# Who asks for a weight, and when: `wo` issued by ScalarE in quarters at the start of a two-layer graph kernel

## The chip, the cores and the metric

The kernel runs on one core of one Trainium2 chip. Its metric is the device time of one execution in microseconds (us), the median of several executions.

## What is computed

The input `x` has 64 batches of 256 rows with 512 features, all float32. `adj` is a 256 x 256 matrix of zeros and ones. Two layers follow each other:

```python
# layer 0: masked attention, 8 heads of 64, then residual and layer norm
q, k, v = (x @ Wq + bq), (x @ Wk + bk), (x @ Wv + bv)        # each (b, 256, 8, 64)
scores  = einsum('bqhd,bkhd->bhqk', q, k) / sqrt(64) + (1 - adj) * -1e9
out     = einsum('bhqk,bkhd->bqhd', softmax(scores), v) @ Wo + bo
x       = layernorm(x + out)
# layer 1: neighbours' sum, one weight, then residual and layer norm
y       = einsum('nm,bmd->bnd', adj, x)
x       = layernorm(x + y @ weight + bias)
```

## The kernel before, in words

**Pairs of batches.** The 64 batches are worked through as 32 pairs. A tile of a pair holds 128 partitions by 512 float32 values. All names below carry the pair, so `x(1, 2)` is the third feature block of pair 1.

**Products in three digits.** A float32 product is made out of three passes over cut numbers in the `fp32r` form. Each operand is split into `high` (a ScalarE copy with a scale), `low` and `diff` (two VectorE operations, L123 and L124 for weights, L288 and L289 for x), and for weights and keys one more ScalarE scaling of `low` (L127, L393). A block of a product is then 4 x 3 = 12 matmuls at L338. `ring_high`, `ring_rest` and `ring_scale` do this for the k-th quarter of a weight; the results go into the pool `wr`, which has six buffers, three for each stage.

**Stages of weights.** `STAGES` lists which digits are in the ring and in what order: the second half of the heads of `wq` and `wk` for pair 0 (`qk1`), then `wv` (`v`, the third weight), then the first half of `wq` and `wk` for pair 1 (`qk0`), and from there on the stages of each pair. The digits of a weight are made once, written to DRAM by GpSimd (`keep`, L132), and read back by GpSimd for each later pair (`load_w`, L110).

**Order of work.** PE, DVE, ACT and POOL run in the order that the program writes out by hand. `start()` is the part that the change touches. It turns pair 0's x on TensorE, makes the products of queries and keys, then `scores(0, 0)` (matmuls L454, exps L469), the products of `v`, `values(0, 0)`, `scores(0, 1)`, and `bv_wo`. A step such as `(ring_rest, "v", 0, 0)` in a list puts its instructions on its engines at that place.

**bv_wo** (L240) multiplies the bias `bv` with `wo` once, so that it can be added to `bo`: four matmuls of 32 columns, one for each quarter of `wo`, each written as two instructions. ScalarE copies the result (L242). `with_bv` (matmul L247, addition L248) adds it to the `bo` tile. After `bv_wo` come two `begun` products, which need only `high` digits, and the products of queries and keys of pair 1 out of the `qk0` digits. `values(0, 1)` (L410, L420) and `scores(1, 0)` follow.

**Loads at the start.** SP issues nearly all of them, in this order: x of pair 0 (L176), columns of `wk` and `wq` (L169), `adj` (L193), `wv` in four parts (L196), x of pair 1 in sixteen parts of 64 KB (L81), `wo` in four quarters of 256 KB (L203, tile `hl`), the biases `bo` and `b1` spread over all partitions (L91), then x of pair 2 and the residual rows (`load_r`, L86). ScalarE issues the first columns of `wq` and the small biases.

**Semaphores of transfers.** In the built program the transfers of SP and ScalarE share eight semaphores, dealt in rotation. A transfer is issued once the previous one with its semaphore has landed.

**adj** is turned by TensorE (`adj_t`, L227), copied into `adjT` by VectorE (L228), and tested once for values other than zero and one (`test_adj`, L232 to L234). **The next rows** are x of pair 1, turned by VectorE (`x_t`, L276).

Of the kernel before, what the change touches and what calls it, by code (L numbers as in the profile page):

```python
# [8 lines left out]
F32 = mybir.dt.float32  # L9
# [6 lines left out]
P = 128  # L16
# [13 lines left out]
def tile_adj_resnorm(tc, x, adj, wq, bq, wk, bk, wv, bv, wo, bo, w1, b1, out):  # L30
    good = fast(tc, x, adj, wq, bq, wk, bk, wv, bv, wo, bo, w1, b1, out)
    with tc.If(good < P):
        general(tc, x, adj, wq, bq, wk, bk, wv, bv, wo, bo, w1, b1, out)


def fast(tc, x, adj, wq, bq, wk, bk, wv, bv, wo, bo, w1, b1, out):
# [6 lines left out]
    nc = tc.nc  # L43
    B, N, D = x.shape
    HD = D // H
    DC = D // P
    NC = N // P
    NP = B // 2
    HF = D // 2
# [12 lines left out]
    two = pool("two", 2)  # L62
# [8 lines left out]
    RAW, SCRATCH, W, UNCUT, BEGUN = {}, {}, {}, {}, {}  # L71
# [3 lines left out]
    def load_x(p, i):  # L75

        if p < NP:

            t = XC[p, i] = two.tile([P, D], F32, name="o" if p == 1 and i > 1 else "x")
            for q in range(4):  # L80
                nc.sync.dma_start(t[q * 32:(q + 1) * 32].rearrange("i (m j) -> i m j", j=32), xb[p, i, q])  # L81
# [7 lines left out]
    def on_all(b, name):  # L89
        t = cpool.tile([P, D], F32, name=name)  # L90
        nc.sync.dma_start(t, b.partition_broadcast(P))  # L91
        return t
# [103 lines left out]
        nc.sync.dma_start(RAW["v", k], wv[k * P:(k + 1) * P])  # L196
    for i in range(4):
        load_x(1, i)
    for k in range(DC):
        if k % 2 == 0:  # L200
            raw_o = two.tile([P, 2, D], F32, name="hl")
        RAW["o", k] = raw_o[:, k % 2]
        nc.sync.dma_start(RAW["o", k], wo[k // 2 * HF:(k // 2 + 1) * HF].rearrange("(h a i) e -> a h i e", h=4, a=2)[k % 2])  # L203
    bo_s, b1_s = on_all(bo, "bo"), on_all(b1, "b1")

    def small_ones():

        nc.gpsimd.memset(power, -0.5)
        nc.gpsimd.memset(first_of_32, 0.0)
        for d in range(DC):  # L210
            nc.gpsimd.memset(first_of_32[d * 32:d * 32 + 1], 1.0)

    def load_l():
        t = two.tile([P, DC, D], F32, name="r")
        nc.sync.dma_start(t, w1.rearrange("(c p) e -> p c e", p=P))
        for k in range(DC):
            RAW["l", k] = t[:, k]
# [223 lines left out]
    def scores(p, g, between=[]):  # L441
        if not 0 <= p < NP:
            return
        for b in range(2):
            for kc in range(NC):

                sc = [banks.tile([P, 2, N], F32, name="ps") for s in range(2)]
                keys = slice(b * N + kc * P, b * N + (kc + 1) * P)
                for a in range(2):
                    digits = (1, 0, 2) if (p, g) != (0, 0) else (0,)  # L450
                    for i in digits:
                        for s in range(2):
                            r = slice(s * HD, (s + 1) * HD)
                            nc.tensor.matmul(sc[s][:, a, :], K[p, g][r, a, i, keys], Q[p, g][r, a, i, b * N:(b + 1) * N],  # L454
                                             start=i == digits[0], stop=i == digits[-1])
                if (p, g) == (NP - 1, 1):

                    names = (("x", two), ("high", four), ("low", four), ("diff", four))
                    name, pool_of = names[2 * b + kc]
                    e = [pool_of.tile([P, 2, N], F32, name=name) for _ in range(2)]  # L460
                    whole = []
                else:
                    e = one.tile([P, 2, 2, N], F32, name=f"e{2 * b + kc}")
                    whole, e = [e.rearrange("p s a n -> p (s a) n")], [e[:, s] for s in range(2)]
                E[p, g, b, kc] = e, whole
                if (b, kc) == (1, 1):
                    do(*between)
                for s in range(2):
                    nc.scalar.activation(e[s], sc[s], AF.Exp, scale=(RHO if (p, g) != (0, 0) else 1.0) * qscale)  # L469
# [15 lines left out]
    def masks(p, g, b):  # L485
        return [(masked, p, g, b, 0), (masked, p, g, b, 1), *([(summed, p, g, b)] if (p, g) != (NP - 1, 1) else [])]
# [145 lines left out]
    def do(*tasks):  # L632
        for t in tasks:
            for f, *args in (t if isinstance(t, list) else [t]):
                f(*args)
# [54 lines left out]
    def steps_of(*args):  # L690

        h, r, s = ([(f, *args, k) for k in range(4)] for f in (ring_high, ring_rest, ring_scale))
        return h[:2], r[:1] + h[2:3] + r[1:2] + h[3:], r[2:3] + s[:1] + r[3:] + s[1:2], s[2:]

    def start():
        make_identity(nc, ident)
        do(*((x_first, i) for i in range(4)), (biases,), *((x_high, 0, i) for i in range(4)), (small_ones,))
        qk1, v = (steps_of(*stage) for stage in STAGES[:2])
        high, rest, scale = ([(f, "qk0", 1, k) for k in range(DC)] for f in (ring_high, ring_rest, ring_scale))
        do((block, "q", 0, 0), (x_rest, 0, 0), (x_rest, 0, 1), qk1[0], (block, "k", 0, 0), (x_rest, 0, 2), (x_rest, 0, 3), qk1[1],  # L700
           (block, "q", 0, 1), qk1[2], v[0], (block, "k", 0, 1), (x_t, 1, 0), (x_t, 1, 1), (adj_t,), qk1[3])
        scores(0, 0)
        do(v[1], masks(0, 0, 0), (block, "q", 0, 2), v[2], (qk_high, "q", 0, 2), (qk_rest, "q", 0, 2), v[3],
           (block, "k", 0, 2), (x_high, 1, 0), (x_high, 1, 1), (qk_high, "k", 0, 2), (qk_rest, "k", 0, 2), masks(0, 0, 1),
           (block, "q", 0, 3), (k_low, 0, 2), (qk_high, "q", 0, 3), (qk_rest, "q", 0, 3), (x_rest, 1, 0), (x_t, 1, 2),
           (block, "k", 0, 3), (stage_end, 0), (qk_high, "k", 0, 3), (qk_rest, "k", 0, 3), (x_rest, 1, 1), (x_t, 1, 3), high[:2],
           (block, "v", 0, 0), (x_high, 1, 2), high[2:], (k_low, 0, 3), (block, "v", 0, 1), (x_rest, 1, 2), (test_adj,),
           (block, "v", 0, 2), (x_high, 1, 3), (x_rest, 1, 3), (block, "v", 0, 3), (stage_end, 0), (load_r, 0), (load_l,))
        values(0, 0)
        scores(0, 1)  # L710
        do((bv_wo,), rest[:2], scale[:1], rest[2:3], scale[1:2], rest[3:], scale[2:])
        qk0 = [(f, name, 1, j) for j in range(2) for name in "qk" for f in (qk_high, qk_rest)]
        m = masks(0, 1, 0) + masks(0, 1, 1)
        do((begun, "q", 1, 0), (begun, "k", 1, 0), (block, "q", 1, 0), m[:4], qk0[:2], (block, "k", 1, 0), m[4:5], qk0[2:4], m[5:],
           (block, "q", 1, 1), (k_low, 1, 0), qk0[4:6], (o_high, 0, 0, 0), (o_high, 0, 1, 0), (o_rest, 0, 0, 0),
           (with_bv,), (block, "k", 1, 1), qk0[6:], (stage_end, 0), (k_low, 1, 1), (o_rest, 0, 1, 0))
# [45 lines left out]
    with tc.manual_schedule(engines={PE, DVE, ACT, POOL}):  # L762
        start()
        first(1, steps_of("o", 0))
        second(1)
        load_r(1)
        for w in range(2, NP - 1):
            first(w)
            second(w)
        ending()  # L770
# [188 lines left out]
```

## Time and profile before

| What | Value |
|---|---|
| median of 3 runs | 2397.47 us (2393.38 to 2397.6) |
| profiled execution | 2397.81 us |
| its span in the profile | 2395.8 us |
| mean granted TensorE clock | 0.998 |
| TensorE (PE) busy | 2376.4 us, 99% |
| weight loads (PEld) busy | 1908.5 us, 80% |
| VectorE (DVE) busy | 1990.7 us, 83% |
| ScalarE (ACT) busy | 1503.4 us, 63% |
| GpSimd (POOL) busy | 440.8 us, 18% |

The span runs from the first to the last instruction; the profiled execution's own time has some 2 us more around it. Busy shares are means over the whole span. A wait shows as idle time ahead of an instruction, and the trace names what ended it.

### The profile page before, as it was taken

Reading aid. Unit: us, or ns where it says so; the run is one execution under the profiler, and the core shown is the slowest. Engines: PE = TensorE matmul, PEld = TensorE weight load, DVE = VectorE, ACT = ScalarE, POOL = GpSimd, SP = SyncE. Lnnn points to the kernel's source line nnn. Section 1 sums busy time; section 2 is a strip of 40 time slices with the busy share of each in tenths; the row PEclk is TensorE's granted clock in tenths of the full one; section 3 lists DMA queues with packets and bytes.
Section 4 is the critical chain, followed back from the end, with each engine's and each line's share of the span. In section 5 each row is a group of like instructions: output and inputs, shape, how many; then the busy total and the mean of one; then the engine's idle time right before and its main releaser. Section 6 shows DMA issues by size and latency. Waiting matters only on the chain.

```text
span 2395.8 us, 42996 instructions
## 1 busy us (share of the span) xinstructions
PE 2376.4 (99%) x16925; PEld 1908.5 (80%) x16925; DVE 1990.7 (83%) x3311; ACT 1503.4 (63%) x2793; POOL 440.8 (18%) x751
## 2 busy tenths in 40 slices
PE   8999999999999999999999999999999999999998
PEld 6788887887878888788887788887888878888777
DVE  7888888898888888888888889888888888888867
ACT  6566566665665666656666566566566665665656
POOL 1121112111111211111111111111121111111121
PEclk9999999999999999999999999999999999999999
DMA  9888788777897777877778877789777887787782
GB/s 290 272 275 251 253 264 295 239 231 259 255 303 247 224 267 255 274 261 239 245 257 264 285 241 235 255 254 310 240 226 265 255 283 259 229 256 258 255 268 68
DMA packets 373091, 608.69 MB, mean 254 GB/s; under 512 B 271500, under 2 KB 275092, under 8 KB 312596
## 3 DMA queue, kind: packets, MB, share of 16 engines
q0 software_dynamic: 70544, 499.15, 56.9%
q1 hardware_dynamic: 301632, 106.34, 20.5%
q8 instruction: 135, 2.21, 0.4%
q14 instruction: 72, 0.59, 0.1%
q10 hardware_dynamic: 708, 0.40, 0.1%
HBM read 551.29 MB, written 49.28 MB: 251 GB/s over the span
## 4 chain that ended last, share of the span: by engine, by line
PE 97%; DMA 2%; SPq 1%; DVE 0%; ACT 0%; issue 0%; POOLq 0%; ACTq 0%
PE ps L338 72%; PE ps L420 9%; PE ps L454 8%; PE ps L614 5%; PE ps L410 3%; DMA hl<-in_L_gnn_Wo_dram 1%; SPq L81 1%; DMA vc<-in_adj_dram 0%; DMA low<-in_x_dram 0%; SPq L203 0%; PE ps L240 0%; PE ps L564 0%; SPq L169 0%; ACT waste L516 0%; PE ps L247 0%
## 5 line engine op out<-in xcount | busy, mean ns | idle before, releaser
L372 ACT ACTIVATE uncut<-ps,numbers 128x512 f32<-128x512 f32 x252 | 173.8, 690 | 275.9 <-PE ps L338 220.1
L475 DVE TENSOR_TENSOR e<-e,adjT 128x1024 f32<-128x1024 f32 x252 | 299.3, 1219 | 0.2 <-ACT e L469 0.2
L338 PE MATMUL ps<-low,wr 128*128 128x512 f32 x992 | 271.4, 395 | 0.0
L338 PE MATMUL ps<-wr,sl 128*128 128x512 f32 x1008 | 270.6, 390 | 0.1
L338 PE MATMUL ps<-wr,sh 128*128 128x512 f32 x1008 | 269.8, 389 | 0.0
L338 PE MATMUL ps<-wr,sd 128*128 128x512 f32 x1008 | 269.4, 389 | 0.0
L338 PE MATMUL ps<-high,wr 128*128 128x512 f32 x992 | 267.0, 391 | 0.0
L338 PE MATMUL ps<-diff,wr 128*128 128x512 f32 x992 | 265.0, 389 | 0.0
L522 POOL TENSOR_TENSOR ln<-ln,numbers 128x2 f32<-128x2 f32 x127 | 140.4, 1105 | 666.7 <-DVE ln L521 615.3
L469 ACT ACTIVATE e<-ps 128x512 f32<-128x512 f32 x504 | 253.0, 626 | 8.9 <-PE ps L454 8.9
L516 ACT ACTIVATE waste<-r,ln 128x512 bf16<-128x512 f32 x255 | 183.4, 719 | 104.7 <-DVE ln L509 98.5
L420 PE MATMUL ps<-e,v 128*32 128x256 f32 x4032 | 229.1, 379 | 0.0
L537 ACT ACTIVATE r<-r,ln 128x512 f32<-128x512 f32 x254 | 193.2, 809 | 55.2 <-DMA x<-in_x_dram 31.4
L338 PEld LDWEIGHTS ps<-wr,sh 128*128 128x128 f32 x1008 | 189.3, 188 | 39.9
L338 PEld LDWEIGHTS ps<-high,wr 128*128 128x128 f32 x992 | 186.6, 188 | 42.7 <-issue 1.7
L338 PEld LDWEIGHTS ps<-wr,sd 128*128 128x128 f32 x1008 | 189.2, 188 | 39.5 <-DMA wr<-o 0.2
L338 PEld LDWEIGHTS ps<-diff,wr 128*128 128x128 f32 x992 | 186.2, 188 | 39.1
L338 PEld LDWEIGHTS ps<-wr,sl 128*128 128x128 f32 x1008 | 186.9, 188 | 38.2 <-issue 0.4
L384 DVE SCALAR_TENSOR_TENSOR qT<-qT,uncut 128x512 fp32r<-128x512 f32 x126 | 86.7, 688 | 154.3 <-ACT qT L377 154.2
L454 PEld LDWEIGHTS ps<-qT,kT 64*128 64x128 f32 x3056 | 187.8, 187 | 26.4 <-PE ps L420 12.3
L338 PEld LDWEIGHTS ps<-low,wr 128*128 128x128 f32 x992 | 177.8, 188 | 35.1 <-PE ps L338 0.2
L454 PE MATMUL ps<-qT,kT 64*128 64x256 f32 x3056 | 201.4, 285 | 0.0
(165 smaller groups left out, 4152.9 us busy)
## 6 DMA issues: line engine op xcount, KB each, us to landing
wr<-qk POOLq DMA_DIRECT2D x183, 1024.0 KB, 7.8
wr<-v POOLq DMA_DIRECT2D x93, 1024.0 KB, 6.7
wr<-o POOLq DMA_DIRECT2D x90, 1024.0 KB, 8.1
wr<-l POOLq DMA_DIRECT2D x90, 1024.0 KB, 8.5
r<-in_x_dram SPq DMA_DIRECT2D x32, 1024.0 KB, 12.3
out_dram<-r SPq DMA_DIRECT2D x62, 512.0 KB, 2.9
x<-in_x_dram SPq DMA_DIRECT2D x488, 64.0 KB, 5.7
qk<-wr POOLq DMA_DIRECT2D x6, 1024.0 KB, 7.1
```

The source lines that it names most:

```text
L338: nc.tensor.matmul(pm, *pairs[k][i], start=i == 0 and k == 0, stop=i == n - 1 and k == DC - 1)
L372: nc.scalar.activation(to, pm, AF.Identity, bias=bias[:, j:j + 1], scale=scale)
L384: nc.vector.scalar_tensor_tensor(low, high.bitcast(F32), -RHO, UNCUT.pop((name, p, j)), op0=OP.mult, op1=OP.add)
L410: nc.tensor.matmul(at[h * 32:(h + 1) * 32, b, :], ones, chunk[h], start=i == 0, stop=i == len(sm) - 1)
L420: nc.tensor.matmul(at[h * 32:(h + 1) * 32, a, :], V[p, b][:, kc, col:col + 32], E[p, g, b, kc][0][h % 2][:, h // 2, :], start=kc == 0, sto ...
L454: nc.tensor.matmul(sc[s][:, a, :], K[p, g][r, a, i, keys], Q[p, g][r, a, i, b * N:(b + 1) * N], start=i == digits[0], stop=i == digits[-1])
L469: nc.scalar.activation(e[s], sc[s], AF.Exp, scale=(RHO if (p, g) != (0, 0) else 1.0) * qscale)
L475: nc.vector.tensor_tensor(e, e, mask[:, kc:kc + 1, :].to_broadcast([P, e.shape[1], N]), op=OP.mult)
L516: nc.scalar.activation(waste, R[p][b][:, c], AF.Square, bias=t[0][:, c:c + 1], accum_out=t[1][:, c:c + 1])
L522: nc.gpsimd.tensor_tensor(t[2], t[1], power[:, cs], op=OP.pow)
L537: nc.scalar.activation(r[:, :cut], r[:, :cut], AF.Identity, scale=scale, bias=bias)
L614: nc.tensor.matmul(pm[:, j, :], t[:, i, mc, j * P:(j + 1) * P], adjT[:, mc, :], start=mc == 0 and i == 0, stop=mc == NC - 1 and i == 1)
```

## The change

The quarters of `wo` are no longer issued by SP between x of pair 1 and the biases. A new step `load_o` issues one quarter from ScalarE's queue; four such steps stand in `start()`. In VectorE's order, the digits of the first quarter of `wv` go ahead of the copy of `adj`, the transpose of x(1, 1) goes behind the digits of the second quarter, and `test_adj` moves from behind x(1, 2)'s digits to ahead of the keys' third block, `(block, "k", 0, 2)`. In the new kernel `load_o` stands at L208 to L212, and the lines behind it are one higher than before (L338 becomes L339).

```diff
-    for k in range(DC):
-        if k % 2 == 0:
-            raw_o = two.tile([P, 2, D], F32, name="hl")
-        RAW["o", k] = raw_o[:, k % 2]
-        nc.sync.dma_start(RAW["o", k], wo[k // 2 * HF:(k // 2 + 1) * HF].rearrange("(h a i) e -> a h i e", h=4, a=2)[k % 2])
     bo_s, b1_s = on_all(bo, "bo"), on_all(b1, "b1")
...
+    def load_o(k):
+        if k % 2 == 0:
+            RAW["o"] = two.tile([P, 2, D], F32, name="hl")
+        RAW["o", k] = RAW["o"][:, k % 2]
+        nc.scalar.dma_start(RAW["o", k], wo[k // 2 * HF:(k // 2 + 1) * HF].rearrange("(h a i) e -> a h i e", h=4, a=2)[k % 2])
...
-        do((block, "q", 0, 0), (x_rest, 0, 0), (x_rest, 0, 1), qk1[0], (block, "k", 0, 0), (x_rest, 0, 2), (x_rest, 0, 3), qk1[1],
-           (block, "q", 0, 1), qk1[2], v[0], (block, "k", 0, 1), (x_t, 1, 0), (x_t, 1, 1), (adj_t,), qk1[3])
+        do((load_o, 0), (block, "q", 0, 0), (x_rest, 0, 0), (x_rest, 0, 1), qk1[0], (load_o, 1), (block, "k", 0, 0), (x_rest, 0, 2), (x_rest, 0, 3),
+           qk1[1], (load_o, 2), (block, "q", 0, 1), qk1[2], v[0], (block, "k", 0, 1), (x_t, 1, 0), v[1][:1], (load_o, 3),
+           (adj_t,), qk1[3])
         scores(0, 0)
-        do(v[1], masks(0, 0, 0), (block, "q", 0, 2), v[2], (qk_high, "q", 0, 2), (qk_rest, "q", 0, 2), v[3],
+        do(v[1][1:], (x_t, 1, 1), masks(0, 0, 0), (block, "q", 0, 2), v[2], (qk_high, "q", 0, 2), (qk_rest, "q", 0, 2), v[3], (test_adj,),
            (block, "k", 0, 2), (x_high, 1, 0), (x_high, 1, 1), (qk_high, "k", 0, 2), (qk_rest, "k", 0, 2), masks(0, 0, 1),
...
-           (block, "v", 0, 0), (x_high, 1, 2), high[2:], (k_low, 0, 3), (block, "v", 0, 1), (x_rest, 1, 2), (test_adj,),
+           (block, "v", 0, 0), (x_high, 1, 2), high[2:], (k_low, 0, 3), (block, "v", 0, 1), (x_rest, 1, 2),
```

## The prediction, made before the changed kernel ran

> **What bounds it now.** First the page: TensorE is busy 99% of the span, and the chain that ended last is TensorE for 97%. Two per cent of that chain is DMA, and its largest piece is `wo` (tile `hl`).
>
> ```profile
> PE 2376.4 (99%) x16925; PEld 1908.5 (80%) x16925; DVE 1990.7 (83%) x3311; ACT 1503.4 (63%) x2793; POOL 440.8 (18%) x751
> ...
> PE 97%; DMA 2%; SPq 1%; DVE 0%; ACT 0%; issue 0%; POOLq 0%; ACTq 0%
> ```
>
> So look where TensorE waits: the waits of TensorE in 0 to 90 us name one large one, and the chain in order of time (start, length) shows its place.
>
> ```profile
> PE ps L240 <- DMA hl<-in_L_gnn_Wo_dram: 6.5, 1, 6.5
> PE ps L260 <- DMA low<-in_x_dram: 4.1, 2, 3.8
> ...
> 30.48 32.98 DMA hl<-in_L_gnn_Wo_dram
> 63.45 0.04 issue
> 63.50 1.91 PE ps L240 x2
> 65.41 8.90 PE ps L338 x36
> 74.31 0.86 PE ps L247 x2
> 75.17 2.76 PE ps L338 x12
> ```
>
> The fourth quarter of `wo` is issued at 30.48 us and lands 33 us later; `bv_wo` (L240) has done three quarters and waits for it. The timeline of TensorE (start, length, names, idle time before), then the windows of 3 us (TensorE busy first, its clock in the third column from the end), give the price.
>
> ```profile
> 55.98 1.06 PE L240 MATMUL ps<-hl,numbers 128*32 128x512 f32 x6
> 63.50 1.91 PE L240 MATMUL ps<-hl,numbers 128*32 128x512 f32 x2 [6.46 <-DMA hl<-in_L_gnn_Wo_dram]
> ...
> 77.86 1.07 PE L410 MATMUL ps<-sm,ones 128*32 128x256 f32 x16
> ```
>
> ```profile
> 57.00:60.00 3.00, 0.04 (x3) 0.00 (x0) 2.93 (x6) 0.96 (x2) 0.00 (x0) 0.95 0.41 132
> 60.00:63.00 3.00, 0.00 (x0) 0.00 (x0) 2.97 (x3) 0.00 (x0) 0.54 (x1) 0.50 0.72 282
> 63.00:66.00 3.00, 2.50 (x4) 0.75 (x5) 1.54 (x2) 0.50 (x2) 0.00 (x0) 0.50 0.70 216
> 66.00:69.00 3.00, 3.00 (x14) 2.46 (x13) 0.00 (x0) 2.17 (x5) 0.53 (x1) 0.92 0.45 78
> ```
>
> The stall also halves TensorE's clock until about 66 us. After 90 us the waits view names none of TensorE at all, so time saved here reaches the end.
>
> **The Trainium skill.** "TensorE: Matmul & The Clock Gate", Part 1 (the HAM clock gate): an idle window of about 3.4 us gates the array to half clock, and as long a busy one frees it. The trace agrees: 0.50 in 60 to 66 us, 1.00 after 69. "DMA: Bandwidth & Descriptors", section on queues, rings and completion order: SP and ACT own one queue row each, and every DMA engine goes round the rows packet by packet. From 30 to 57 us the trace gives GpSimd's q0 72.6% and SP's q1 19.6%, which fits `wo` crawling behind 3 MB of weight copies. Same page, "Issuing engines are not separate DMA queues": another issuer brings no bandwidth. No run yet shows the effect of that. Same page, on the anatomy of one DMA: semaphore waits happen on the issuing sequencer; here SP's issues stand so.
>
> **The change, part by part.**
>
> *Gain.* From `bv_wo` at 55.98 to `values(0,1)` at 77.86 TensorE takes 21.88 us. Its work there: eight `bv_wo` matmuls, 1.06 for six plus 0.35 for two, 1.4; 48 matmuls L338 at 0.227 (a block of 12 is 2.72, from the starts of its groups), 10.9; L247 0.86. Sum 13.2, so 8.7 us are lost: 6.46 idle, 1.91 - 0.35 = 1.56 and 12.52 - 11.76 = 0.76 at half clock.
>
> *When `wo` lands now.* ScalarE issues the quarters at about 12, 15, 18 to 19 and 23 us, against 28.4 to 30.5. Even with the old 33 us the last lands at 57, where it is needed; 25 to 45 us is likelier, as far less stands ahead of it in its row.
>
> *What is late next.* ScalarE's four scalings of the qk0 digits (L127) follow its eight exps and the `bv_wo` copy. Exps end at 57.96, the copy at 58.55, then 0.55 each: 59.1, 59.65, 60.2, 60.7. TensorE, after eight `begun` matmuls, wants the first at 59.2 and the fourth at 59.9: 0.8 lost. VectorE's share of the digits is done at 59.7. From 59.2, with 0.8 of stall, the 40 matmuls left (9.1) and L247 (0.86) bring `values(0,1)` to 70.0 instead of 77.86: 7.86 gained.
>
> *VectorE behind it.* It loses its 6.67 us idle time before L384 (64.54 to 71.21). Contiguous work of 9.77 us from there to 80.98 now ends at 74.2; ScalarE's `k_low` adds 0.63, so 74.8. `scores(1,0)` starts 4.46 after `values(0,1)`, at 74.5, and wants the second half of the keys 0.4 later. A tie: 0 to 0.3, I take 0. Further on VectorE had 1.47 idle at 96.3, enough.
>
> *ScalarE's four issues.* Each is a queue instruction of 0.3 to 0.7 us (ACTq's old ones 0.26 to 0.58, SP's of 256 KB 0.43 to 1.05), plus a wait. Hardware-queue transfers share eight semaphores in rotation, and an issue waits for its semaphore's previous transfer. The built program shows these waits: quarter 0 for the second half of `wq` (landed 11.86), quarter 1 for `wv` 0 (14.7), quarter 2 for `wv` 3 (17.5), quarter 3 for quarter 1. Queued behind each is the copy out of a TensorE product, and TensorE waits for that copy. ScalarE's room:
>
> ```profile
> 12.19 0.69 ACT L372 ACTIVATE qT<-ps,numbers 128x512 f32<-128x512 f32 x1 [1.44 <-PE ps L338]
> ...
> 15.62 0.69 ACT L372 ACTIVATE kT<-ps,numbers 128x512 f32<-128x512 f32 x1 [1.71 <-PE ps L338]
> ...
> 19.06 0.69 ACT L372 ACTIVATE qT<-ps,numbers 128x512 f32<-128x512 f32 x1 [1.71 <-PE ps L338]
> ...
> 22.49 0.69 ACT L372 ACTIVATE kT<-ps,numbers 128x512 f32<-128x512 f32 x1 [0.67 <-PE ps L338]
> ...
> 24.11 4.00 ACT L469 ACTIVATE e<-ps 128x512 f32<-128x512 f32 x8
> ```
>
> The first two fit to 0.2 us (11.86 and 14.7, plus 0.5). For the third, 512 KB of new traffic at the windows' 370 GB/s push `wv` 3 by 1.4 to 18.9; issued by 19.4 it makes the copy at 19.06 late by 0.35, less than the 0.67 idle before 22.49. The score matmuls feel it only if `wv` 3 lands after 19.3. The fourth delays the exps by 0.5; TensorE needs the first bank back at 26.47, so 1.6 may go. I book 0.2 for all four; bounds 0 and 2. Below nothing is excluded here: nothing on this path becomes earlier.
>
> *SP's queue.* It loses four issues (28.41 to 31.52), so `bo`, `b1`, x(2,..) and R follow sooner. But semaphores are dealt anew: x(1,0)'s last part waits for `wv` 1, x(1,1)'s third part for quarter 0, x(1,2)'s last for quarter 2, `bo` for quarter 3. `bo` is wanted by `with_bv` at 72.2 (it landed at 64.1 before), x(1,2) at 43.9: nothing booked. GpSimd's copies keep their order and meet 1 MB more traffic earlier; their landings have over 5 us of room before TensorE's use.
>
> *VectorE's order.* The transpose of x(1,1), which stood 2.86 idle until 23.42, goes behind the digits of `wv` 1 and `adj`'s copy. With x landing some 2 later, x(1,0)'s transpose comes at 21.5, one digit pair (1.33) to 23.5, `adj` to 24.2; the last scores need its bank at 25.4: covered, 1.2 to spare. The `adj` test (three operations, 1.0) moves from 49.1 into the 1.51 idle at 34.87, and frees 1.0 at 50 that ends at `vc` (53.65) anyway: at most 0.15 of it counts. All else moved costs nothing, because TensorE runs without a gap from 26.5 to 57.
>
> *Sum.* 7.86 - 0.2 = 7.7. Against the profiled execution (2397.81; span 2395.8, 2.0 around it) that is 2390.1; the median, 2397.47, is 0.34 lower, so 2389.8.
>
> **Rivals.** (A) *Less is gained:* the waits on `wv` 3 or quarter 1 hold ScalarE 1 to 3 us past its room, or VectorE decides at the keys. For it: the room is 0.7 and 1.6. Gain 3 to 6, time 2391.5 to 2394.5. (B) *Slower:* quarter 3's wait for quarter 1 stands ahead of the exps. If quarter 1 needs the 33 us that a quarter took in SP's queue, it lands at 49; the exps start there and not at 25.7 at latest, 23 us of stall against 7.9 saved: about 2413. It decides from a landing after 33 us. Against it: quarter 1 is issued before GpSimd's copies (17.66), in a row of its own. (C) *No change:* quarter 3 lands as late as before, starved by q0, or `bo` behind it holds `with_bv` until the old time: about 2396 to 2398. Against it: it starts 7 us earlier.
>
> **Numbers.** Forecast 0.62, A 0.21, C 0.10, B 0.07. A measurement of this kernel tells some 0.2% (4.8 us) from no change, and one of the three times shown is 2393.38. The forecast's own range is 2387 to 2391.5; with most of A it is 2387 to 2394. Faster by over 0.2% is below 2392.7: the forecast and most of A, 0.78. Same: the rest of A and C, 0.15. Slower: B, 0.07.
>
> **What would show it.** Right: no wait of L241 for `hl`, clock 1.00 throughout 57 to 69, `values(0,1)` near 70.2 (77.86), four DMA issues on ACTq with the copy L373 late by under 0.7, VectorE unbroken from 64 to 74. A gap before the score matmuls (L455) at 23 to 26 us would show A or B; a wait at L241 or before L249 shows C. The prediction is wrong if TensorE gets a new idle stretch over 3 us before 90 us, or the gain is outside 3.5 to 10.5.

## The result: slower, 1.0027 times the time before

The changed kernel takes 2402.87 us (median; 2399.82 to 2407.7) against 2397.47 us in the same set of runs. The ratio is 1.0027, with a 95% interval of 1.0017 to 1.0036: slower by about 4 to 9 us, where 2389.8 was predicted. Its profiled execution, at 2400.37 us (span 2398.4), is among its faster ones, and so shows only 2.6 of these microseconds.

The page first. TensorE's busy time and share have hardly moved, and DMA has gone from the chain that ended last; VectorE has come in.

```profile
PE 2377.4 (99%) x16925; PEld 1909.5 (80%) x16925; DVE 1990.3 (83%) x3311; ACT 1502.3 (63%) x2793; POOL 439.4 (18%) x751
...
PE 96%; DVE 1%; ACT 0%; issue 0%; POOLq 0%; ACTq 0%
```

The waits of TensorE in 0 to 100 us (total, times, longest) name what took the place of `wo`. There is no wait for `hl` any more, and a new one of 7.4 us for `adjT`.

```profile
PE ps L455 <- DVE adjT L229: 7.4, 1, 7.4
...
PE ps L455 <- ACT kT L394: 0.5, 1, 0.5
```

TensorE's timeline gives the places. The last six matmuls of `scores(0,0)` stand still from 25.9 to 33.35; `bv_wo` then runs as one piece of 1.06 us.

```profile
22.65 3.29 PE L455 MATMUL ps<-qT,kT 64*128 64x256 f32 x26
33.35 2.07 PE L455 MATMUL ps<-qT,kT 64*128 64x256 f32 x6 [7.42 <-DVE adjT L229]
...
66.16 1.06 PE L241 MATMUL ps<-hl,numbers 128*32 128x512 f32 x8
...
79.45 1.07 PE L411 MATMUL ps<-sm,ones 128*32 128x256 f32 x16
...
84.99 2.78 PE L455 MATMUL ps<-qT,kT 64*128 64x256 f32 x42 [0.46 <-ACT kT L394]
```

The windows (TensorE busy first, its clock third from the end) show that the half clock moved along with the stall: from 60 to 66 us in the kernel before to 27 to 38 us here.

```profile
27.00:30.00 3.00, 0.00 (x0) 0.00 (x0) 0.00 (x0) 2.44 (x5) 0.53 (x1) 0.65 0.47 132
30.00:33.00 3.00, 0.00 (x0) 0.00 (x0) 2.28 (x4) 1.62 (x4) 0.00 (x0) 0.50 0.91 354
33.00:36.00 3.00, 2.65 (x8) 1.72 (x9) 1.59 (x3) 1.14 (x3) 0.00 (x0) 0.50 0.50 145
...
63.00:66.00 3.00, 3.00 (x52) 2.91 (x48) 2.81 (x6) 2.50 (x5) 0.65 (x2) 1.00 0.62 262
```

`adjT` is late because VectorE, ahead of it, waits 10.86 us for the first rows of pair 1. Its timeline:

```profile
30.69 0.71 DVE L277 STREAM_TRANSPOSE xT<-x 128x512 f32<-128x512 f32 x1 [10.86 <-DMA x<-in_x_dram]
31.32 0.65 DVE L123 SCALAR_TENSOR_TENSOR wr<-wr,high 128x512 fp32r<-128x512 f32 x1
32.01 0.69 DVE L124 SCALAR_TENSOR_TENSOR wr<-wr 128x512 fp32r<-128x512 f32 x1
32.62 0.68 DVE L229 CAST adjT<-ps 128x512 fp32r<-128x512 f32 x1
```

In the kernel before, x(1,0) was turned at 19.86 without a wait and `adj` copied at 24.06:

```profile
19.86 0.71 DVE L276 STREAM_TRANSPOSE xT<-x 128x512 f32<-128x512 f32 x1
...
24.06 0.65 DVE L228 CAST adjT<-ps 128x512 fp32r<-128x512 f32 x1
```

SP's timeline shows the same x in its queue: the eight issues of x(1,0) and x(1,1), before and then after.

```profile
10.49 8.12 SPq L81 DMA_DIRECT2D x<-in_x_dram  x8
```

```profile
11.18 17.00 SPq L81 DMA_DIRECT2D x<-in_x_dram  x8
```

It is not the issues that make x(1,0) late. Its four parts were issued by 16.2 us, against 15.0 before; the last of them landed at 30.66, against 18.85 (a landing is the last update of the transfer's semaphore in the trace).

**The balance**, read from the start of the first sums matmul (L410, after L411) in each `values` block. The table holds the changed kernel and all experiments; x(1,0)'s column shows lateness only where VectorE reaches its transpose early, so not in 8 and 9, where it stands further back. Differences are to the profile of the kernel before, ratios to its runs in the same set (medians 2396.9 to 2397.5).

| Kernel | Time, us | Ratio (95%) | x(1,0) turned at | values(0,0) | values(0,1) | values(1,0) |
|---|---|---|---|---|---|---|
| before | 2397.47 | 1 | 19.9 | 48.46 | 77.86 | 118.25 |
| changed | 2402.87 | 1.0027 (1.0017-1.0036) | 30.7 | +10.17 | +1.58 | +2.31 |
| 1 order alone | 2398.13 | 1.0005 (0.9996-1.0014) | 19.9 | +0.01 | +1.32 | +1.33 |
| 2 issue alone | 2406.69 | 1.0041 (1.0027-1.0055) | 26.4 | +16.25 | +7.66 | +8.86 |
| 3 quarter 3 later | 2403.54 | 1.0026 (1.0015-1.0036) | 33.5 | +12.71 | +4.12 | +4.84 |
| 4 16 columns early | 2399.55 | 1.0009 (1.0000-1.0017) | 20.4 | +0.76 | +2.90 | +3.83 |
| 5 128 columns early | 2397.3 | one run | 20.7 | +1.06 | -0.70 | -0.32 |
| 6 SP, `wo` first | 2406.98 | one run | 38.6 | +15.70 | +7.62 | +9.20 |
| 7 copies later | 2396.07 | 0.9993 (0.9986-1.0000) | 27.8 | +7.78 | -0.81 | -0.16 |
| 8 adj first | 2402.8 | 1.0018 (1.0009-1.0026) | 36.0 | +1.24 | +7.44 | +8.19 |
| 9 the same, quarter 3 later | 2397.42 | 1.0004 (0.9995-1.0013) | 41.7 | +2.28 | -1.62 | -0.90 |
| 10 GpSimd issues | 2392.04 | 0.9975 (0.9965-0.9985) | 20.2 | +0.32 | -8.26 | -7.48 |
| 11 GpSimd's loads later | 2390.56 | 0.9971 (0.9959-0.9984) | 19.9 | -0.05 | -8.65 | -5.84 |
| 12 GpSimd and new order | 2392.09 | 0.9983 (0.9975-0.9992) | 21.1 | +1.61 | -6.95 | -6.26 |

For the changed kernel: 10.17 us are lost before `values(0,0)` (7.42 idle, the rest the half-clock work until about 38 us, 0.17 less for an earlier start). From there to `values(0,1)` 10.17 - 1.58 = 8.59 come back, and the keys take 0.73. Nothing of size changes later.

### The profile page after: what moved, and what is told of

It reads as the page before. It is cut to its first block, busy times and chain, and to the rows that moved or that the text cites. A ratio compares the mean times of both kernels' runs of the same rounds, so it can differ in the third digit from the quotient of the medians.

```text
span 2398.4 us, 42996 instructions
## 1 busy us (share of the span) xinstructions
PE 2377.4 (99%) x16925; PEld 1909.5 (80%) x16925; DVE 1990.3 (83%) x3311; ACT 1502.3 (63%) x2793; POOL 439.4 (18%) x751
## 4 chain that ended last, share of the span: by engine, by line
PE 96%; DVE 1%; ACT 0%; issue 0%; POOLq 0%; ACTq 0%
PE ps L339 71%; PE ps L421 9%; PE ps L455 8%; PE ps L615 5%; PE ps L411 3%; DVE e L476 0%; DVE wr L124 0%; DVE wr L123 0%; PE ps L565 0%; DVE kT L389 0%; DVE qT L387 0%; DVE qT L385 0%; ACT kT L394 0%; DVE kT L385 0%; ACT waste L517 0%
## 5 line engine op out<-in xcount | busy, mean ns | idle before, releaser
L339 PE MATMUL ps<-low,wr 128*128 128x512 f32 x992 | 271.6, 395 | 0.0
L339 PE MATMUL ps<-wr,sl 128*128 128x512 f32 x1008 | 270.6, 390 | 0.1
L339 PE MATMUL ps<-wr,sh 128*128 128x512 f32 x1008 | 269.8, 390 | 0.0
L339 PE MATMUL ps<-wr,sd 128*128 128x512 f32 x1008 | 269.5, 389 | 0.0
L339 PE MATMUL ps<-high,wr 128*128 128x512 f32 x992 | 266.4, 390 | 0.0
L339 PE MATMUL ps<-diff,wr 128*128 128x512 f32 x992 | 265.0, 389 | 0.0
L421 PE MATMUL ps<-e,v 128*32 128x256 f32 x4032 | 229.1, 379 | 0.0
L339 PEld LDWEIGHTS ps<-wr,sh 128*128 128x128 f32 x1008 | 189.3, 188 | 39.9
L339 PEld LDWEIGHTS ps<-wr,sd 128*128 128x128 f32 x1008 | 189.1, 188 | 39.8 <-DMA wr<-o 0.5
L339 PEld LDWEIGHTS ps<-high,wr 128*128 128x128 f32 x992 | 186.2, 188 | 41.8 <-ACT e L470 0.8
L339 PEld LDWEIGHTS ps<-diff,wr 128*128 128x128 f32 x992 | 186.2, 188 | 39.1
L339 PEld LDWEIGHTS ps<-wr,sl 128*128 128x128 f32 x1008 | 186.9, 188 | 38.2 <-issue 0.4
L455 PEld LDWEIGHTS ps<-qT,kT 64*128 64x128 f32 x3056 | 188.6, 188 | 35.0 <-PE ps L421 12.3
L455 PE MATMUL ps<-qT,kT 64*128 64x256 f32 x3056 | 203.3, 286 | 7.9 <-DVE adjT L229 7.4
L339 PEld LDWEIGHTS ps<-low,wr 128*128 128x128 f32 x992 | 177.7, 188 | 35.5 <-ACT wr L127 0.6
```

Source lines behind the costliest of these rows:

```text
L339: nc.tensor.matmul(pm, *pairs[k][i], start=i == 0 and k == 0, stop=i == n - 1 and k == DC - 1)
L421: nc.tensor.matmul(at[h * 32:(h + 1) * 32, a, :], V[p, b][:, kc, col:col + 32], E[p, g, b, kc][0][h % 2][:, h // 2, :], start=kc == 0, sto ...
```

## The experiments

**Theory T:** `wo`'s transfers, moved ahead of or beside x of pair 1, make x late, and VectorE, in its fixed order, passes the lateness on. **Rivals:** S, ScalarE's wait for a quarter decides; R, the new dealing of semaphores makes x late, not the bytes; and that the new order of VectorE is itself to blame.

### 1 and 2: each half of the change alone

Order alone: the kernel before with the changed lists of VectorE, without the four `load_o` steps. Issue alone: the changed kernel with the old order:

```diff
-           (x_t, 1, 0), v[1][:1], (load_o, 3), (adj_t,), qk1[3])
+           (x_t, 1, 0), (x_t, 1, 1), (load_o, 3), (adj_t,), qk1[3])
...
-        do(v[1][1:], (x_t, 1, 1), masks(0, 0, 0),
+        do(v[1], masks(0, 0, 0),
```

> VectorE's new order alone, wo asked for by SP as before. Theory T (wo's bytes in ScalarE's row crowd x(1,0) out) and theory R (the semaphores dealt anew let x(1,0)'s parts be issued later): both say no harm here: x(1,0) is transposed at about 19.9 us, adj copied by 23.6, no wait of the score matmuls for adjT, and the 6 us wait of bv_wo for wo stays: 2395 to 2399 us. If the order itself were the cause of the loss: a wait for adjT and 2402 us or more.

> ScalarE's four issues of wo alone, VectorE's order as before, so both transposes of x(1,*) stand ahead of adj's copy. T and R: x(1,0) comes at about 30 us and x(1,1) at about 37.6, so adj is copied only at about 39 and the score matmuls wait some 13 us instead of 7.4: 2405 to 2410 us. Theory S (ScalarE's wait for quarter 1 ahead of the exps decides): no more than the changed kernel, 2401 to 2404 us.

Order alone is no different from before (5.3 us of wait for `hl` remain). Issue alone is the slower half; from its waits of TensorE:

```profile
PE ps L339 <- DVE adjT L229: 13.8, 1, 13.8
```

Both transposes stand ahead of `adj` in the old order, and x(1,1) was turned only at 40.02. So the issue does the harm, and the new order, which puts x(1,1) behind `adj`, takes away some 4 of its 9 us. S is out here: ScalarE waited less than 1 us for quarter 1 in this run.

### 3: quarter 3 behind the exps

```diff
-           v[1][:1], (load_o, 3), (adj_t,), qk1[3])
+           v[1][:1], (adj_t,), qk1[3])
...
-        do(v[1][1:], (x_t, 1, 1), masks(0, 0, 0),
+        do(v[1][1:], (load_o, 3), (x_t, 1, 1), masks(0, 0, 0),
```

> The changed kernel with its fourth quarter of wo issued behind the eight exps, so that ScalarE no longer stands 4.6 us ahead of the exps. T and R: x(1,0) is as late as before, the score matmuls still wait about 7 us for adjT: 2399 to 2404 us. S: the wait ahead of the exps was the loss, so 2391 to 2395 us.

The time did not fall, and TensorE's wait for `adjT` was 9.3 us. (x(1,0) was turned at 33.5 here and at 26.4 in experiment 2, with the same three quarters of `wo` ahead of it as in the changed kernel: single profiles differ by this much.) In the changed kernel ScalarE does wait, as its timeline shows (a queue instruction, then the next operation with the idle time before it), but beside TensorE's longer wait for VectorE:

```profile
26.98 0.54 ACTq L212 DMA_DIRECT2D hl<-in_L_gnn_Wo_dram  x1
27.56 1.15 ACT L127 ACTIVATE wr<-wr 128x512 fp32r<-128x512 f32 x2 [4.55 <-DMA hl<-in_L_gnn_Wo_dram]
```

### 4 and 5: fewer bytes at the same places

The four early issues keep their places and semaphores, and move 16 or 128 of the 512 columns; the rest follows from ScalarE behind the exps of `scores(0,0)`.

```diff
-        nc.scalar.dma_start(RAW["o", k], wo[k // 2 * HF:(k // 2 + 1) * HF].rearrange("(h a i) e -> a h i e", h=4, a=2)[k % 2])
+        part_o(k, 0, 16)
+
+    def part_o(k, a, b):
+        of = wo[k // 2 * HF:(k // 2 + 1) * HF, a:b].rearrange("(h a i) e -> a h i e", h=4, a=2)[k % 2]
+        nc.scalar.dma_start(RAW["o", k][:, a:b], of)
+
+    def rest_o(k):
+        part_o(k, 16, D)
...
-        do(v[1][1:], (x_t, 1, 1), masks(0, 0, 0),
+        do(v[1][1:], *((rest_o, k) for k in range(4)), (x_t, 1, 1), masks(0, 0, 0),
```

> The changed kernel, but the four early issues fetch 16 of 512 columns each (8 KB instead of 256 KB); the other 496 columns are issued by ScalarE behind the exps. The semaphores that x(1,0)'s and x(1,1)'s issues wait on are the changed kernel's. T: without the 1 MB x(1,0) has landed by about 21 us, no wait for adjT, no wait of bv_wo or a short one: 2388 to 2392 us. R: x(1,0) still comes at 27 to 31 us and the score matmuls wait 4 to 8 us: 2396 to 2403 us.

> The changed kernel with 128 of wo's 512 columns (64 KB of each quarter, 512-byte rows instead of 2-KB rows, as many packets as before) issued by ScalarE at the four early places, the other 384 columns behind the exps of scores(0,0). It stands between the changed kernel (all early, x(1,0) turned at 30.7 us) and the kernel with 16 columns early (turned near 22). Theory of traffic: what delays x(1,0) is the number of wo's bytes that share the transfer engines with it, so its lateness grows with them: worked out in a straight line, x(1,0) is turned at about 24, adj's copy comes near 25.5, and the wait of the score matmuls for it is 0 to 1 us. Rival of turns: ScalarE's row takes one packet for each packet of x whatever its length, so a quarter of the bytes with the same number of packets costs nearly as much: the wait is 5 to 7.5 us. The 16 columns spoke for bytes, but at 64 bytes a packet. Both expect wo's rest behind the exps to hold up x(1,2) and x(1,3) as it did with 496 columns; total 2396 to 2400 by traffic, 2402 or more by turns.

In both, TensorE's wait for `adj` is gone, and x(1,0) is turned when VectorE comes to it, at 20.4 and 20.7. It landed at 19.8 and 20.7, after three early issues (24 and 192 KB in all), which is 0.9 and 1.8 us later than in the kernel before. After three or four whole quarters (the changed kernel and experiments 2, 3, 7, 8 and 9) it landed at 26.4 to 34.5, so 7.5 to 15.6 later. The lateness grows with the bytes; whether in step with them, the spread of single profiles hides. R is refuted, since these issues use the same semaphores, and so is the rival of packet turns, by one run. The gain was lost elsewhere, which the totals expected for 16 columns missed: the rest of `wo`, issued at 27.5 to 33 us, now meets x(1,2) and x(1,3) (tile `o`). The waits of VectorE and TensorE with 16 columns:

```profile
DVE xT L284 <- DMA o<-in_x_dram: 10.2, 1, 10.2
```

```profile
PE ps L428 <- ACT v L371: 9.1, 1, 9.1
```

### 6: the same bytes in SP's own queue

The kernel before with `wo` ahead of x of pair 1; ScalarE issues none of it.

```diff
-    for i in range(4):
-        load_x(1, i)
     for k in range(DC):
...
         nc.sync.dma_start(RAW["o", k], wo[k // 2 * HF:(k // 2 + 1) * HF].rearrange("(h a i) e -> a h i e", h=4, a=2)[k % 2])
+    for i in range(4):
+        load_x(1, i)
```

> The kernel before with wo's four quarters ahead of x of pair 1 in SP's own queue; ScalarE issues none of them. Theory of traffic: wo's 1 MB ahead of or beside x(1,0) delays it whoever asks; at the 280 to 370 GB/s of these windows 1 MB is 2.8 to 3.8 us of traffic, plus SP's four issues, so x(1,0) (19.9 us in the kernel before) is turned at 24 to 27, x(1,1) some 3 later, both ahead of adj's copy in this order: a wait of the score matmuls for adj of 3 to 8 us, no wait for wo at bv_wo, total 2393 to 2399. Rival: only a second row does the harm, because there each small packet of x takes turns with a large one of wo: in one row x is late by no more than the 3 to 4 us of bytes. Told apart by x(1,0)'s transpose: up to 25 for the rival, 27 and later if a row of its own is not what matters.

x(1,0) was turned at 38.63, later than in any other kernel with this order. So a second queue row is not what does the harm: `wo` ahead of x is enough, whether ScalarE or SP asks. That side was named for 27 and later; the total of 2393 to 2399 was missed. `wo`, with x behind it, ran into GpSimd's copies as well: its last quarter, issued by 16.4, landed at 37.27. TensorE had no wait for `adj` here; the same idle VectorE (18.6 us ahead of x(1,0)) reached it through the digits of `wv`, 11.2 us in five waits:

```profile
PE ps L338 <- ACT wr L127: 11.2, 5, 5.8
```

### 7: GpSimd's first copies away

The changed kernel with GpSimd's three `qk1` copies held back until `wv`'s first copy.

```diff
+                if name == "qk1":
+                    LATER.append((name, i, W[stage][i]))
+                    continue
                 keep(name, i, W[stage][i])
+                while LATER and name == "v":
+                    keep(*LATER.pop(0))
```

> The changed kernel, with GpSimd's three copies of qk1's digits (3 MB, issued at 17.9 to 29 us) put behind its first copy of v's digits, so not before about 27 us. If wo's bytes and the copies together make x(1,0) late: x(1,0) and x(1,1) land by 20 and 25 us, quarter 1 by 20, so there is no wait for adjT and none of ScalarE: 2388 to 2393 us. If wo's bytes alone suffice: x(1,0) is still later than 26 us and the score matmuls wait over 4 us: 2396 us or more.

The second expectation was met, by little: x(1,0) was turned at 27.8, TensorE waited 4.04 for `adjT` (7.42 in the changed kernel), and the time is 2396.07. So `wo` alone is enough to make x late. What the copies add cannot be read from x(1,0), which landed at 26.4 to 34.5 in the five kernels that have them. The median is 6.8 us below the changed kernel's, so they do cost time; by which path, one profile does not show.

From 18 to 27 us only two queues were at work. Their shares of the 16 DMA engines (the view of DMA by queue; packets, MB, share):

```profile
q10 hardware_dynamic: 344, 0.68, 22.4%
q1 hardware_dynamic: 2069, 0.26, 19.2%
```

On average the engines were less than half busy while x crawled, and yet some were full. The trace has the start and length of every packet. Of `wo`'s packets, four ran at once for 6.4 of these 9 us and hardly ever five (0.04 us), although up to three quarters were under way; of x's, sixteen and more at once at times. So all quarters of `wo` run on the same four of the sixteen engines, and these were some 90% busy with it (22.4% of sixteen engines is 3.6 engines). x is spread over all sixteen, and a part of it has landed only when its share on those four has, too. Here the parts of x(1,0) landed at 21.29, 24.20, 27.28 and 27.77, the first three quarters of `wo` at 21.26, 24.40 and 27.54.

Experiment 6 shows it in one queue. Of the 512 packets of x's first part, 384, which is three quarters, ran from 21.9 to 22.3 us. Then no packet of x ran for 7.4 us, and the part landed at 37.46, 0.2 us behind the last quarter of `wo`. A packet of `wo` takes 0.084 us (the median in experiment 7), so its 512 packets are 10.8 us of work for four engines: an estimate from these numbers, against 2.8 for 1 MB at 370 GB/s. Why these transfers get four engines, no run settles. Their source is written as four blocks (`h=4`), and a version without that was not run.

### 8 and 9: adj ahead of both transposes

```diff
-           (block, "k", 0, 1), (x_t, 1, 0), v[1][:1], (load_o, 3), (adj_t,), qk1[3])
+           (block, "k", 0, 1), (adj_t,), v[1][:1], (load_o, 3), qk1[3])
...
-        do(v[1][1:], (x_t, 1, 1), masks(0, 0, 0),
+        do(v[1][1:], masks(0, 0, 0),
...
-           (block, "k", 0, 2), (x_high, 1, 0), (x_high, 1, 1),
+           (block, "k", 0, 2), (x_t, 1, 0), (x_t, 1, 1), (x_high, 1, 0), (x_high, 1, 1),
```

The digits of `wv` are thus ahead of the transposes as well; in 9 they stand the same, but `(load_o, 3)` is behind the exps.

> The changed kernel with both transposes of pair 1's x moved behind everything that the first scores need: adj's copy and v's four digits go first, x(1,0) and x(1,1) are turned right ahead of their digits. ScalarE issues wo as in the changed kernel. Theory (x's lateness matters only because adj's copy stands behind it): no wait of the score matmuls for adj, the stall at bv_wo still gone; what is left is ScalarE's wait for quarter 1 (the exps start near 28.6, the first bank comes back near 29.3, TensorE wants it near 26.5): a stall of 2 to 3 us near 26 us and, with wo's stall of 8.7 gone, 2391 to 2394. If ScalarE's wait costs nothing, 2389 to 2391. Rival (the late x is needed itself: its digits stand ahead of pair 0's keys in VectorE's order): the wait only moves, to between 35 and 50 us, of 4 to 8 us, and the total is 2396 to 2402.

> The same with the fourth quarter of wo issued behind the exps of scores(0,0), so that ScalarE does not wait ahead of them. Theory: the stall near 26 us goes as well: 2389 to 2391, 1 to 3 us below the kernel with adj first alone. If ScalarE's wait was covered, the two agree within 1 us. Rival (late x needed itself): 2396 to 2402 again, with a wait between 35 and 50 us.

The wait for `adj` is gone in both, and TensorE runs unbroken over 26 us, also where ScalarE issues quarter 3 ahead of the exps (at 24.18 there). But late x is needed for itself. In 8 it came even later (x(1,1) turned at 50.09), VectorE stood 13.4 us, and TensorE waited further on:

```profile
PE ps L411 <- DVE sm L484: 6.7, 1, 6.7
...
PE ps L421 <- ACT v L364: 4.0, 1, 4.0
```

So the rival named with these runs holds: the wait only moves, in 8 to 50 us and later (at most 50 was named), with a total of 2402.8, just above the rival's 2402. In 9 it is 2.9 us at L421 and 1.5 at L339, where ScalarE's quarter 3 stood until 36.4 for the semaphore of an x part. That eats most of what `wo` gives back.

### 10, 11 and 12: `wo` in time without passing x

Number 10 is the kernel before with `wo` issued by GpSimd behind its third copy, at 25.4 to 27.4. Number 11 leaves `wo` in SP's queue, and moves GpSimd's three loads of `wv`'s digits for pair 1 from before `values(0,0)` to behind `bv_wo`. Number 12 is 10 with VectorE's order of the changed kernel.

```diff
+        nc.gpsimd.dma_start(RAW["o", k], wo[k // 2 * HF:(k // 2 + 1) * HF].rearrange("(h a i) e -> a h i e", h=4, a=2)[k % 2])
...
-           (adj_t,), qk1[3])
+           (adj_t,), qk1[3], *((load_o, k) for k in range(4)))
```

```diff
-        if ended[0] + 1 < len(STAGES) and ended[0] > 1:
+        if ended[0] + 1 < len(STAGES) and ended[0] > 2:
...
-        do((bv_wo,), rest[:2],
+        do((bv_wo,), (load_w, STAGES[3]), rest[:2],
```

> The kernel before, with wo's four quarters issued by GpSimd behind its third weight copy (at about 25 us) instead of by SP; VectorE's order as before. Theory T (who shares the DMA engines with whom, and when, decides; the copies' queue gets most of them): x(1,0) and x(1,1) land as before (no wait for adjT), wo lands by 40 us in the favoured queue, bv_wo does not wait: 2387 to 2391 us, the 8 us that the changed kernel was meant to save. Rival (x(1,2) and x(1,3) then starve as they did when wo went late by ScalarE): VectorE waits for tile o at 44 to 58 us and TensorE stalls 3 to 9 us: 2392 to 2399 us.

> The kernel before, with GpSimd's three loads of v's digits for pair 1 (3 MB, issued at 39 to 47 us, used at 96) moved behind scores(0,1), so issued from 53 us on. T: with that traffic away wo lands by about 45 us and bv_wo does not wait: 2387 to 2391 us. Rival (wo is late by what stands ahead of it in SP's own queue, not by the weight traffic): it lands after 57 us as before and the time stays at 2395 to 2399 us.

> wo asked for by GpSimd behind its third weight copy, as in the faster version tried alone, and VectorE in the changed kernel's order. With wo on time and x of pair 1 on time, nothing waits on VectorE in the first 60 us except at the key blocks, so the order is worth nothing of its own: no wait for wo at bv_wo, none for adj, values(0,1) near 69.6, total 2391 to 2393, equal within 1 us to GpSimd's issue with the old order (2392.0). Rival (the order was the useful half and frees VectorE ahead of the keys): the 0.5 us wait of the second scores for the keys goes as well and the total falls to 2390 to 2391.5.

All three beat both kernels, the one before by 0.17 to 0.29%. TensorE's timeline in number 10:

```profile
56.31 1.06 PE L241 MATMUL ps<-hl,numbers 128*32 128x512 f32 x8
...
69.60 1.07 PE L411 MATMUL ps<-sm,ones 128*32 128x256 f32 x16
```

The quarters landed at 37.0 to 39.0, and x(1,0) kept its 20.2. The total, 2392.04, lies a microsecond above the range expected, without the stall that its rival named. Here the packets of `wo`, 4 KB each, ran up to sixteen and more at once, not four: issued by GpSimd, it is spread over the engines. Number 10 thus changes who asks as well as when, and does not tell the two apart. Number 11 shows what had starved `wo` in the kernel before: with SP's queue as it was and only GpSimd's loads moved, `bv_wo` runs without a wait at 55.93. The last quarter landed at 53.31, later than the 45 expected, and in time. The biases behind it land at 54.0 instead of 64.1. Its profiled execution, the longest of six (2395.3), pays part of it back at 75 to 150 us (VectorE waits 5.9 us for x of pair 2); so moving the loads moves the collision. Number 12 equals 10: with x on time the new order is worth nothing.

## Why the prediction was wrong, point by point

- **The gain was right in its own window.** `bv_wo` to `values(0,1)` was to shrink from 21.88 by 7.86; it took 79.45 - 66.16 = 13.29, a gain of 8.59. The difference is the 0.8 us of ScalarE's scalings booked as a stall; with everything shifted by 10 us they were in time. That all of it reaches the end was too much: number 10, without the new stall, is 8.26 ahead at `values(0,1)`, 6.31 at the end of its profiled execution and 5.4 in the median.
- **ScalarE's four issues** took 0.54 to 0.64 us each, as booked. The copies at 12.19 and 15.62 came 0.56 and 0.22 later, the third not: `wv`'s last part landed at 17.8, and not at the 18.9 reckoned from 370 GB/s. The fourth issue's wait for quarter 1 was 4.55 us, far over the 0.5 booked, but ran beside TensorE's wait for VectorE; experiment 3 shows that taking it away gains nothing there.
- **The step that failed is the cost of `wo`'s traffic to x, in "VectorE's order":** "With x landing some 2 later, x(1,0)'s transpose comes at 21.5 ... covered, 1.2 to spare." x was 11 later, the transpose came at 30.7, `adj` at 32.6. The stall of 7.42 us and its half clock cost 10.17. The 2 us are what three quarters of `wo` take at 370 GB/s, the rate that it used for `wv`, as if they ran on all engines and x lost only the time of those bytes. The packets show that `wo` runs on four engines, 10.8 us of work for 1 MB, and that x, which needs these four too, lands behind it (experiments 6 and 7): 0.9 and 1.8 us late with 16 and 128 columns early, 7.5 to 15.6 with whole quarters, 19.6 (38.44 against 18.85) with all four in front.
- **Where the profile could have warned.** The prediction saw SP's x parts only as landing times. In the kernel before, eight of them sat 8.12 us in SP's queue, close to the start of GpSimd's copies, and VectorE already waited 2.86 for the last. Whatever is pushed ahead of them had no cover of 1.2 us but the start of a crowd. The question "what will that collide with" was asked for `wo` and not for x, which `wo` passed. And the 33 us of the last quarter were put down to the crowd alone, though the packets were in that trace, too: from 48 to 63.4 us the 2-KB packets of SP's queue (`wo` and the biases) ran four or fewer at once for 14.5 of 15.4 us.
- **The order** was judged nearly neutral. Alone it is (1.0005). Beside the issue it is worth 2406.69 - 2402.87 = 3.8 us, because `adj` then waits for one block of x and not for two.
- **VectorE behind the keys** was a tie of 0 to 0.3: TensorE waited 0.46 there, and 0.73 was lost in all.
- **The rivals.** B gave the right side by the wrong mechanism: quarter 1 landed at 26.95, not after 33, and did not decide. The new idle stretch before L455 at 23 to 26 us was named as the sign against the forecast, and that is where it is; it was ended by VectorE, which no rival named.
- **The skill's sentence** on issuing engines, in "DMA: Bandwidth & Descriptors", "Issuing engines are not separate DMA queues", says that another issuer brings no bandwidth. For ScalarE and SP the runs agree: in the changed kernel (x(1,0) landed at 30.66) and in 6 (38.44), `wo` from either queue delays x. For GpSimd it is not the whole account: the same bytes ran on four engines from ScalarE and on up to sixteen from GpSimd (number 10).
- **Left open.** The profile shows 2.6 of the 4 to 9 us that the runs give; that x lands later still in other executions is likely, and not shown. Nor is it settled what GpSimd's copies add, and whether a `wo` that is spread over all engines could be asked for early by ScalarE without harm.

## What to carry to other kernels

Before a transfer is moved ahead, list the transfers that it passes and the engine that waits for each in program order; their room is what the move may spend. Then look at how many packets of the moved transfer run at once: here four, so that it took far longer than its bytes at the full rate, and everything spread over all engines had to wait for those four. A low mean share of the DMA engines hides this. A transfer that is late because a crowd is on the DMA engines is helped by moving it to a gap, or by moving a part of the crowd that is wanted later; here each gave 5 to 7 us (the first by another issuer as well), while pushing it in front of the loads gave a stall of the same size elsewhere. A stall that goes with a slip of 10 us upstream looks like a success in its own window: compare the starts of the same blocks, not only the waits.

## What was not expected of the hardware

- SP's issue of one 64 KB part of x takes 0.49 us in a quiet stretch and up to 10.0 us in a crowded one (experiment 6, at 19.09): the queue instruction itself is longer, and what stands behind it on SP slips too.
- One load can fill four DMA engines and leave the others mostly idle: x of pair 1 moved 0.26 MB in 9 us beside 0.68 MB of `wo` with the DMA engines 42% busy on average (experiment 7).
- The same 1 MB ran four packets at once from ScalarE's and SP's queues (experiments 7 and 6), and up to sixteen and more from GpSimd's (number 10).
